# A state-space scan stage: step sizes formed in the product's PSUM bank, side jobs moved to other units, more products shared with GpSimd

## The chip, the core and the metric

The kernel runs on one core of a Trainium2 chip. A core has a matrix engine (TensorE, PE in the profile; PEld is its weight load), a vector engine (VectorE, DVE), an activation engine (ScalarE, ACT), GpSimd (POOL) and SyncE (SP), which here only issues DMAs. Each works through its own queue in order and waits on semaphores for the others. SBUF is the large on-chip memory; PSUM has eight banks of 2 KB per partition, and TensorE writes only there. The metric is the device time of one execution in microseconds; here the median of three was 3026.71 (3026.7 to 3028.8).

## The reference

The program is a decoder of two layers over 16 blocks of 128 tokens with 512 features; each of its six parts is followed by a residual sum and a layer norm. The change touches only the first part, a selective state-space scan over every block:

```python
A = -jnp.exp(A_log)                                                        # 512 x 16
dt = jax.nn.softplus(jnp.einsum('bld,ed->ble', x, dt_proj_w) + dt_proj_b)  # step sizes
bc = jnp.einsum('bld,ed->ble', x, x_proj_w) + x_proj_b
Bs, Cs = (bc[..., :d_state], bc[..., d_state:])                            # 16 and 16

def step(h, inputs):
    xt, dtt, Bt, Ct = inputs
    dA = jnp.exp(dtt[..., None] * A)
    dBx = (dtt * xt)[..., None] * Bt[:, None, :]
    h = dA * h + dBx
    y = jnp.einsum('bdn,bn->bd', h, Ct)
    return (h, y)
...
return jnp.einsum('bld,md->blm', y, out_proj_w) + out_proj_b
```

The parts after it (cross attention, ternary feed-forward, causal attention, a second cross attention, a mixture of experts) are the same in both kernels.

## The kernel before, in words

`stage_ssm` does the scan with features on the partitions: 512 features are four chunks (KC = 4) of 128 partitions, and two blocks of 128 tokens form a pair of TQ = 256 tokens. There are eight pairs, and in each 16 units, one for each state n; `units` counts u = 16 p + n. A tile of a unit is 128 x 1024 in 32 bits. One unit is

- `widths_in`: SP fetches `BC`, the rows of B and C of the state, spread over all partitions (four units ahead; six buffers)
- `decays`: ACT writes exp(dt A) into a PSUM tile `h` of two banks (a small copy of zeros and four activations, one unit ahead; two buffers, so four banks)
- `terms`: GpSimd forms `dBx` = dtx * B (two units ahead; three buffers)
- `scan`: DVE scans along the tokens. In an own unit it scans `h` in place and multiplies with C into `hC` (three buffers). In a shared unit (`shared`) it scans into `hs` in SBUF (two buffers), and GpSimd multiplies with C
- `add`: TensorE adds hC or hs, turned, into two banks `py` (eight transposes against the identity); for an own unit one unit later, for a shared unit two units later

Around them each pair does side jobs at fixed units n. For the next pair: `widths` (product `pb` for B and C, one bank), `widths_out` (ACT adds the bias, a DMA takes it to HBM), and for each half h of the features `step_product` (product `pd` in a bank), `step_exp`, `step_one`, `step_log` (ACT), `step_rest` (DVE) and `step_sum` (GpSimd), which form softplus as max(z, 0) + log(1 + e^-|z|) with a correction of the rounding of 1 + e^-|z|. For the pair behind: `sums_out` (ACT copies `py` to yT at n = 0), `turn_back` (PE), `turned_out` (ACT), `output` (PE product `po`) and `output_sum` (DVE). And `keys_values`: 64 products `pkv` on TensorE of keys and values for later stages, each copied by ACT and sent to HBM one unit later (`keys_values_out`). pb, pd, pt, po and pkv share the last two banks, "A" and "B", one tile each at a time.

In the loop over units everything is recorded through `pinned` (line 66 in the profile), which keeps the program's order on each engine: the order within an engine is that in which the code stands. The code before the loop, which forms the step sizes of the first pair, is ordered by the scheduler of the framework except for what `keep` holds.

Of the kernel before, what the change touches and what calls it, by code (L numbers as in the profile page):

```python
# [20 lines left out]
P = 128  # L21
# [86 lines left out]
def stage_ssm(k):  # L108
# [9 lines left out]
    with ExitStack() as ctx:  # L118
# [36 lines left out]
        for h in range(2):  # L155
            es = slice(2 * h * P, (2 * h + 2) * P)
            nc.scalar.dma_start(dtw[:, :, es], a["dtwT"][:, es].rearrange("(c p) e -> p c e", p=P))
        for whole, row in zip(wholes, rows):

            left = wk.tile([65, D], F32, tag="BC", name="left", bufs=6)  # L160
            nc.gpsimd.tensor_copy(row, whole)
            nc.gpsimd.tensor_tensor(left, whole, row, ALU.subtract)
            for r in (32, 64):
                nc.gpsimd.tensor_copy(row[r : r + 1], left[r : r + 1])
            nc.gpsimd.tensor_tensor(left[64:65], left[64:65], row[64:65], ALU.subtract)
            nc.gpsimd.tensor_copy(row[64:65], left[64:65])

# [25 lines left out]

        def step_product(st, h, which="A"):


            st.pd[h] = bank(which, [P, 2, TQ], "pd")
            for e in range(2):
                at = (2 * h + e) * P
                for c in range(KC):  # L200
                    q.nc.tensor.matmul(st.pd[h][:, e], dtw[:, c, at : at + P], st.xT[:, c], start=c == 0, stop=False)
                q.nc.tensor.matmul(st.pd[h][:, e], rows[0][:, at : at + P], ones, start=False, stop=True)

        def step_exp(st, h, room=None):
            if room is None:
                v = wk.tile([P, 2, TQ], F32, tag="sp_v", name="sp_v", bufs=1)
                u = wk.tile([P, 2, TQ], F32, tag="sp_u", name="sp_u", bufs=1)
            else:
                v, u = room[:, 0:2], room[:, 2:4]
            st.vu[h] = v, u  # L210
            q.nc.scalar.activation(v, st.pd[h], AF.Abs)
            q.nc.scalar.activation(v, v, AF.Exp, scale=-1.0)

        def step_one(st, h):
            v, u = st.vu[h]
            q.nc.scalar.activation(u, v, AF.Identity, bias=1.0)

        def step_rest(st, h):
            v, u = st.vu[h]
            q.nc.vector.scalar_tensor_tensor(v, u, 1.0, v, ALU.subtract, ALU.subtract)  # L220
            q.nc.vector.scalar_tensor_tensor(v, st.pd[h], 0.0, v, ALU.max, ALU.subtract)

        def step_log(st, h):
            q.nc.scalar.activation(st.dt[:, 2 * h : 2 * h + 2], st.vu[h][1], AF.Ln)

        def step_sum(st, h):
            hs = slice(2 * h, 2 * h + 2)
            q.nc.gpsimd.tensor_tensor(st.dt[:, hs], st.dt[:, hs], st.vu[h][0], ALU.add)
            q.nc.gpsimd.tensor_tensor(st.dtx[:, hs], st.dt[:, hs], st.xT[:, hs], ALU.mult)

# [89 lines left out]

        shared = lambda u: u % 8 in (1, 4, 6)

# [26 lines left out]
        for p, st in enumerate(states):  # L349
            st.p, st.h, st.BC, st.dBx, st.hC, st.pd, st.vu, st.yT, st.pt, st.y = p, {}, {}, {}, {}, {}, {}, {}, {}, {}  # L350
        first = states[0]
        widths(first, xT0)
        widths_out(first)
        room = wk.tile([P, KC, TQ], F32, tag="hC", name="room", bufs=3)
        for step in (step_product, step_exp, step_one, step_rest, step_log, step_sum):
            for h in range(2):
                step(first, h, *{step_product: ["AB"[h]], step_exp: [room if h else None]}.get(step, []))
        for _ in range(2):
# [12 lines left out]
        for u, (st, n) in enumerate(units):  # L371
# [65 lines left out]
            if n in (7, 11) and nxt:  # L437
                step_log(nxt, n // 11)
        last = states[-1]
# [1646 lines left out]
```

## Time and profile before

| What | Value |
| --- | --- |
| median of three runs | 3026.71 us |
| profiled execution, and its span | 3033.7 us, 3031.8 us |
| busy in the span | PE 97%, DVE 63%, POOL 49%, ACT 45% |
| scan stage | first scan at 29.66 us, last pair's yT at 512.74 us |
| chain that ended last, whole span | PE 67%, DVE 13%, ACT 3%, POOL 1% |
| groups of the scan stage | `decays` activation x508, 477 ns; own scans x80, 2290 ns; shared scans x48, 2282 ns; `hC` products x79, 1225 ns |
| `dt` and `dtx` on GpSimd (`step_sum`) | x14 each, 1271 and 1270 ns |

The profile is that of one execution. Busy time counts an engine's instructions; idle time is put down to the event that ended it. A group's row names the line, the engine, the operation, output <- input, the shape and the count, then busy microseconds and the mean in nanoseconds of one, then idle time before them and what ended it. A timeline row has the start, the duration in microseconds (merged where instructions of one kind follow each other), and in brackets the idle time before it.

### The profile page before, as it was taken

The numbers are of one execution on the slowest core, as the hardware profiler recorded it, in microseconds if no ns is written. First come the engines' busy times: TensorE is split into PE (matmuls) and PEld (weight loads), VectorE is DVE, ScalarE is ACT, GpSimd is POOL, SyncE is SP. The second block draws the span as 40 slices with busy tenths as digits, with TensorE's granted clock in tenths as the row PEclk, the third lists the DMA queues.
The fourth block names the chain that finished last, engine by engine and source line by source line (L and its number), as shares of the span: only waits on it lengthen the run. The fifth ranks groups of instructions, "written<-read, shape, count | busy, mean of one in ns | idle before, by whom it ended". The sixth has DMA issues, their size and how long they took to land.

```text
span 3031.8 us, 40699 instructions
## 1 busy us (share of the span) xinstructions
PE 2927.2 (97%) x13744; PEld 1830.9 (60%) x13744; DVE 1920.5 (63%) x4221; ACT 1356.5 (45%) x3315; POOL 1490.4 (49%) x1274
## 2 busy tenths in 40 slices
PE   8999999999999999999999999999999999999998
PEld 6666665455555555555787556666566666666665
DVE  6989998766776676665887897567643322242224
ACT  5776775333343343345344797655433322222221
POOL 8999996534334334332333663356435553333331
PEclk9999999999999999999999999999999999999999
DMA  6654444880000000024000200234357665555541
GB/s 199 205 138 126 121 126 135 266 285 14 8 11 11 8 11 11 8 66 143 1 1 1 70 1 8 64 115 164 136 174 241 221 226 164 165 192 165 164 150 61
DMA packets 171603, 331.58 MB, mean 109 GB/s; under 512 B 22078, under 2 KB 80958, under 8 KB 169852
## 3 DMA queue, kind: packets, MB, share of 16 engines
q1 hardware_dynamic: 126988, 219.91, 23.9%
q0 software_dynamic: 19200, 64.16, 6.3%
q10 hardware_dynamic: 25200, 44.84, 3.9%
q8 instruction: 111, 1.82, 0.2%
q14 instruction: 104, 0.85, 0.1%
HBM read 244.57 MB, written 137.43 MB: 126 GB/s over the span
## 4 chain that ended last, share of the span: by engine, by line
PE 67%; DVE 13%; ACT 3%; POOL 1%; issue 1%; DMA 1%; SPq 0%; another core or an unknown queue 0%; DVEq 0%; ACTq 0%; POOLq 0%
PE y L1830 8%; PE pu L1813 7%; PE pg L1813 7%; PE pq L676 7%; PE po L796 6%; PE po L1008 4%; PE ao L785 3%; PE sc L745 3%; PE pt L536 2%; PE pg L988 2%; PE pu L988 2%; PE pT L773 1%; PE ptx L536 1%; PE pkv L66 1%; PE pw L1482 1%
## 5 line engine op out<-in xcount | busy, mean ns | idle before, releaser
L765 POOL TENSOR_TENSOR pr<-pr,sm 128x512 f32<-128x512 f32 x128 | 135.4, 1058 | 369.2 <-DVE sm L764 273.8
L66 POOL TENSOR_TENSOR dBx<-dtx,BC 128x1024 f32<-128x1024 f32 x126 | 298.6, 2394 | 1.0 <-DMA BC<-bcd 0.4
L1813 PE MATMUL pg<-gu,xgT 128*128 128x352 f32 x784 | 297.1, 461 | 1.4 <-ACT act L1816 1.4
L1813 PE MATMUL pu<-gu,xgT 128*128 128x352 f32 x784 | 296.9, 460 | 0.0
L758 ACT ACTIVATE pr<-sc,mx,sf 128x256 f32<-128x256 f32 x256 | 142.2, 560 | 332.8 <-DVE mx L751 304.7
L1817 DVE SCALAR_TENSOR_TENSOR act<-pu,row,act 128x352 f32<-128x352 f32 x98 | 57.1, 582 | 358.4 <-PE pu L1813 339.2
L1830 PE MATMUL y<-dn,aT 128*128 128x512 f32 x588 | 268.3, 592 | 0.0
L1858 POOL TENSOR_TENSOR x<-got,x 128x512 f32<-128x512 f32 x120 | 151.7, 1270 | 225.8 <-DMA got<-results,gidx 224.6
L66 ACT ACTIVATE h<-dt,negA 128x254 f32<-128x254 f32 x508 | 242.2, 477 | 16.9
L796 PE MATMUL po<-w,aT 128*128 128x512 f32 x512 | 233.1, 593 | 1.9 <-DVE aT L790 1.9
L676 PE MATMUL pq<-w,xT 128*128 128x512 f32 x512 | 230.8, 593 | 0.6 <-DVE m L642 0.6
L1851 POOL DMA_INDIRECT got<-results,gidx x120 | 116.2, 969 | 227.6 <-DMA results<-yo 200.5
L66 DVE TENSOR_TENSOR_SCAN h<-h,dBx 128x1024 f32<-128x1024 f32 x80 | 183.2, 2290 | 34.3 <-ACT h L66 24.9
L1813 PEld LDWEIGHTS pu<-gu,xgT 128*128 128x128 f32 x784 | 149.3, 191 | 83.0 <-issue 0.5
L1816 ACT ACTIVATE act<-pg 128x352 f32<-128x352 f32 x98 | 45.5, 464 | 304.5 <-PE pg L1813 265.3
L1813 PEld LDWEIGHTS pg<-gu,xgT 128*128 128x128 f32 x784 | 141.6, 191 | 65.1 <-ACT act L1816 1.9
L647 POOL TENSOR_TENSOR m<-m,m 128x512 f32<-128x512 f32 x96 | 122.5, 1276 | 111.3 <-DVE m L642 108.0
L66 PE MATMUL pkv<-w,cT 128*128 128x512 f32 x384 | 171.6, 593 | 1.4 <-ACT y L66 1.1
L1842 DVE COPY yo<-y 128x512 f32<-128x512 f32 x90 | 62.2, 691 | 165.4 <-PE y L1830 157.9
L1830 PEld LDWEIGHTS y<-dn,aT 128*128 128x128 f32 x588 | 104.1, 190 | 100.8 <-issue 94.2
L1805 ACT COPY xgT<-ptx 128x512 f32<-128x512 f32 x98 | 57.4, 586 | 235.9 <-PE ptx L536 221.4
L998 POOL TENSOR_TENSOR lo<-sg,hi 128x512 fp32r<-128x512 f32 x64 | 84.2, 1316 | 155.4 <-ACT hi L997 155.3
(413 smaller groups left out, 6792.0 us busy)
## 6 DMA issues: line engine op xcount, KB each, us to landing
bucket<-zeros SPq DMA_DIRECT2D x96, 388.0 KB
row<-bucket SPq DMA_DIRECT2D x90, 388.0 KB
BC<-bcd SPq DMA_DIRECT2D x128, 256.0 KB
results<-yo ACTq DMA_DIRECT2D x90, 256.0 KB
gu<-in_moe_guT SPq DMA_DIRECT2D x16, 1408.0 KB
x_k<-kv ACTq DMA_DIRECT2D x32, 256.0 KB
x_v<-kv ACTq DMA_DIRECT2D x32, 256.0 KB
v<-x_v SPq DMA_DIRECT2D x32, 256.0 KB
```

What stands on the lines that cost most here:

```text
L66: return self.tc.keep_in_program_order(call(*args, **kw))
L647: nc.gpsimd.tensor_tensor(m1, m1, m2, ALU.add)
L676: nc.tensor.matmul(ps, src[:, c], w[c], start=c == 0, stop=c == KC - 1)
L758: nc.scalar.activation(pr[:, j], st.sc[g, i][:, j], AF.Exp, scale=st.sf[:, h : h + 1], bias=st.mx[g, i][:, j : j + 1], accum_out=sm[:, j : ...
L765: nc.gpsimd.tensor_tensor(pr, pr, sm.unsqueeze(2).to_broadcast([P, 2, 2 * P]), ALU.mult)
L796: nc.tensor.matmul(st.po, aT[:, j], k.wo[h // 8][:, h % 8], start=h == 0, stop=h == G * J - 1)
L988: nc.tensor.matmul(p[:, e], w[:, c, at : at + P], sn.qT[:, :, c], start=c == 0, stop=c == KC - 1)
L1008: nc.tensor.matmul(sn.po[i], part[:, e, i * P : (i + 1) * P], k.fd[hc // 8][:, hc % 8], start=hc == 0 and part is parts[0], stop=hc == 15 ...
L1813: nc.tensor.matmul(ps, u.xT[:, c], gu[:, c, lo : lo + I], start=c == 0, stop=c == KC - 1)
L1830: self.nc.tensor.matmul(u.y, u.aT[:, c], u.w[1][:, c], start=c == 0, stop=c == 2)
L1851: nc.gpsimd.indirect_dma_start(out=got[:, :], out_offset=None, in_=k.results[h][g][0:end, :], in_offset=bass.IndirectOffsetOnAxis(ap=self. ...
L1858: nc.gpsimd.tensor_tensor(k.x[b], got, k.x[b], ALU.add)
```

## The change

`step_exp` keeps m = max(z, 0) and u = |z| in SBUF and writes e^-|z| over the product in its PSUM bank; the sums that follow stay in that bank. `step_sum` moves from GpSimd to DVE, and `step_out` copies dt from the bank to SBUF with ACT. Seven of 16 units are shared instead of six, at other places. Side jobs stand at other units, and the banks of `keys_values` change with them. `step_log` now follows `step_one` in its unit or two units later. Before the loop, one of the two bias rows is split on DVE, 26 products of ones are issued on TensorE, and the first pair's step sizes are formed in four quarters (`first_steps`). The core of the diff:

```diff
+        warm = bank("B", [P, 2, TQ], "warm")
+        for _ in range(26):
+            nc.tensor.matmul(warm[:, 0], ones[:, 0:P], ones, start=True, stop=True)
-        for whole, row in zip(wholes, rows):
+        for engine, whole, row in zip((nc.vector, nc.gpsimd), wholes, rows):
...
-            nc.gpsimd.tensor_copy(row, whole)
-            nc.gpsimd.tensor_tensor(left, whole, row, ALU.subtract)
+            engine.tensor_copy(row, whole)
+            engine.tensor_tensor(left, whole, row, ALU.subtract)
...
-        def step_product(st, h, which="A"):
+        def step_product(st, h):
-            st.pd[h] = bank(which, [P, 2, TQ], "pd")
+            st.pd[h] = bank("A", [P, 2, TQ], "pd")
...
-        def step_exp(st, h, room=None):
-            if room is None:
-                v = wk.tile([P, 2, TQ], F32, tag="sp_v", name="sp_v", bufs=1)
-                u = wk.tile([P, 2, TQ], F32, tag="sp_u", name="sp_u", bufs=1)
-            else:
-                v, u = room[:, 0:2], room[:, 2:4]
-            st.vu[h] = v, u
-            q.nc.scalar.activation(v, st.pd[h], AF.Abs)
-            q.nc.scalar.activation(v, v, AF.Exp, scale=-1.0)
+        def step_exp(st, h):
+            m = wk.tile([P, 2, TQ], F32, tag="sp_m", name="sp_m", bufs=1)
+            u = wk.tile([P, 2, TQ], F32, tag="sp_u", name="sp_u", bufs=1)
+            st.mu[h] = m, u
+            q.nc.scalar.activation(m, st.pd[h], AF.Relu)
+            q.nc.scalar.activation(u, st.pd[h], AF.Abs)
+            q.nc.scalar.activation(st.pd[h], u, AF.Exp, scale=-1.0)
 
         def step_one(st, h):
-            v, u = st.vu[h]
-            q.nc.scalar.activation(u, v, AF.Identity, bias=1.0)
+            q.nc.scalar.activation(st.mu[h][1], st.pd[h], AF.Identity, bias=1.0)
+
+        def step_log(st, h):
+            q.nc.scalar.activation(st.dt[:, 2 * h : 2 * h + 2], st.mu[h][1], AF.Ln)
 
         def step_rest(st, h):
-            v, u = st.vu[h]
-            q.nc.vector.scalar_tensor_tensor(v, u, 1.0, v, ALU.subtract, ALU.subtract)
-            q.nc.vector.scalar_tensor_tensor(v, st.pd[h], 0.0, v, ALU.max, ALU.subtract)
-
-        def step_log(st, h):
-            q.nc.scalar.activation(st.dt[:, 2 * h : 2 * h + 2], st.vu[h][1], AF.Ln)
+            m, u = st.mu[h]
+            q.nc.vector.scalar_tensor_tensor(st.pd[h], u, 1.0, st.pd[h], ALU.subtract, ALU.subtract)
+            q.nc.vector.tensor_tensor(st.pd[h], m, st.pd[h], ALU.subtract)
 
         def step_sum(st, h):
             hs = slice(2 * h, 2 * h + 2)
-            q.nc.gpsimd.tensor_tensor(st.dt[:, hs], st.dt[:, hs], st.vu[h][0], ALU.add)
-            q.nc.gpsimd.tensor_tensor(st.dtx[:, hs], st.dt[:, hs], st.xT[:, hs], ALU.mult)
+            q.nc.vector.tensor_tensor(st.pd[h], st.dt[:, hs], st.pd[h], ALU.add)
+            q.nc.vector.tensor_tensor(st.dtx[:, hs], st.pd[h], st.xT[:, hs], ALU.mult)
+
+        def step_out(st, h):
+            q.nc.scalar.copy(st.dt[:, 2 * h : 2 * h + 2], st.pd[h])
+
+        def first_steps(st, c, room):
+            h, e = divmod(c, 2)
+            if e == 0:
+                st.pd[h] = bank("AB"[h], [P, 2, TQ], "pd")
+            pd, (m, u) = st.pd[h][:, e], [r[:, c] for r in room]
+            at = c * P
+            for i in range(KC):
+                nc.tensor.matmul(pd, dtw[:, i, at : at + P], st.xT[:, i], start=i == 0, stop=False)
+            nc.tensor.matmul(pd, rows[0][:, at : at + P], ones, start=False, stop=True)
+            nc.vector.tensor_scalar(m, pd, 0.0, None, ALU.max)
+            nc.scalar.activation(u, pd, AF.Abs)
+            nc.scalar.activation(pd, u, AF.Exp, scale=-1.0)
+            nc.scalar.activation(u, pd, AF.Identity, bias=1.0)
+            nc.scalar.activation(st.dt[:, c], u, AF.Ln)
+            nc.vector.scalar_tensor_tensor(pd, u, 1.0, pd, ALU.subtract, ALU.subtract)
+            nc.vector.tensor_tensor(pd, m, pd, ALU.subtract)
+            nc.vector.tensor_tensor(st.dt[:, c], st.dt[:, c], pd, ALU.add)
+            nc.gpsimd.tensor_tensor(st.dtx[:, c], st.dt[:, c], st.xT[:, c], ALU.mult)
...
-        shared = lambda u: u % 8 in (1, 4, 6)
+        shared = lambda u: u % 16 in (4, 6, 7, 8, 12, 13, 14)
...
-        room = wk.tile([P, KC, TQ], F32, tag="hC", name="room", bufs=3)
-        for step in (step_product, step_exp, step_one, step_rest, step_log, step_sum):
-            for h in range(2):
-                step(first, h, *{step_product: ["AB"[h]], step_exp: [room if h else None]}.get(step, []))
+        room = [wk.tile([P, KC, TQ], F32, tag="hC", name="room", bufs=3) for _ in range(2)]
+        for c in range(KC):
+            first_steps(first, c, room)
...
+                if n in (8, 14):
+                    step_out(nxt, n // 14)
...
+                if n in (6, 12):
+                    step_log(nxt, n // 12)
...
-            if n in (4, 8) and back:
-                output_sum(back, n // 8)
-            if n in (7, 11) and nxt:
-                step_rest(nxt, n // 11)
-            if n in (8, 13) and nxt:
+            if n in (6, 9) and back:
+                output_sum(back, n // 9)
+            if n in (6, 12) and nxt:
+                step_rest(nxt, n // 12)
+            if n in (7, 13) and nxt:
                 step_sum(nxt, n // 13)
...
-                if n in (3, 7):
-                    output(back, n // 7)
+                if n in (5, 8):
+                    output(back, n // 8)
...
-            at = {5: "B", 9: "B", 11: "B", 12: "A", 13: "B", 14: "A", 15: "B"}
+            at = {2: "B", 6: "B", 9: "B", 11: "B", 12: "B", 14: "B", 15: "A"}
             if not back:
-                at |= {0: "A", 1: "B", 3: "B", 7: "B"}
+                at |= {0: "B", 1: "A", 4: "B", 7: "B"}
             if not nxt:
-                at |= {2: "A", 4: "A", 8: "A"}
+                at |= {4: "A", 7: "A", 10: "A"}
...
-            if n in (7, 11) and nxt:
-                step_log(nxt, n // 11)
```

`step_exp` stays at n = 5 and 9, `step_one` at 6 and 10, `step_product` at 4 and 8, `widths` at 2, `widths_out` at 3.

More of the change, by code (lines that the diff above doesn't have):

```diff
@@ L157, in stage_ssm @@
             nc.scalar.dma_start(dtw[:, :, es], a["dtwT"][:, es].rearrange("(c p) e -> p c e", p=P))
-        for whole, row in zip(wholes, rows):
+        warm = bank("B", [P, 2, TQ], "warm")
+        for _ in range(26):
+            nc.tensor.matmul(warm[:, 0], ones[:, 0:P], ones, start=True, stop=True)
+        for engine, whole, row in zip((nc.vector, nc.gpsimd), wholes, rows):
             left = wk.tile([65, D], F32, tag="BC", name="left", bufs=6)
-            nc.gpsimd.tensor_copy(row, whole)
-            nc.gpsimd.tensor_tensor(left, whole, row, ALU.subtract)
+            engine.tensor_copy(row, whole)
+            engine.tensor_tensor(left, whole, row, ALU.subtract)
             for r in (32, 64):
-                nc.gpsimd.tensor_copy(row[r : r + 1], left[r : r + 1])
-            nc.gpsimd.tensor_tensor(left[64:65], left[64:65], row[64:65], ALU.subtract)
-            nc.gpsimd.tensor_copy(row[64:65], left[64:65])
+                engine.tensor_copy(row[r : r + 1], left[r : r + 1])
+            engine.tensor_tensor(left[64:65], left[64:65], row[64:65], ALU.subtract)
+            engine.tensor_copy(row[64:65], left[64:65])
         negA = cst.tile([P, KC, NS], F32, name="negA")
@@ L349, in stage_ssm @@
         for p, st in enumerate(states):
-            st.p, st.h, st.BC, st.dBx, st.hC, st.pd, st.vu, st.yT, st.pt, st.y = p, {}, {}, {}, {}, {}, {}, {}, {}, {}
+            st.p, st.h, st.BC, st.dBx, st.hC, st.pd, st.mu, st.yT, st.pt, st.y = p, {}, {}, {}, {}, {}, {}, {}, {}, {}
         first = states[0]
```

## The prediction

> **What bounds it now.** The change lies in the first 513 us, so I read the busy times by stretch first, the groups by shape of that stretch second, and the timelines of ACT, DVE and PE last.
>
> ```profile
> core 0: us, PE busy (x) PEld busy (x) DVE busy (x) ACT busy (x) POOL busy (x), PEclk, DMA share, GB/s
> 300.00:400.00 100.00, 92.93 (x482) 63.13 (x483) 90.80 (x55) 71.47 (x164) 92.63 (x44) 1.00 0.42 129
> 400.00:500.00 100.00, 96.86 (x506) 66.32 (x506) 91.27 (x54) 70.19 (x162) 93.34 (x42) 1.00 0.42 119
> ```
>
> Three engines are over 90% busy; none of them alone is the bound.
>
> ```profile
> L66 POOL TENSOR_TENSOR dBx<-dtx,BC 128x1024 f32<-128x1024 f32 x126 | 298.6, 2394 | 1.0 <-DMA BC<-bcd 0.4
> L66 POOL TENSOR_TENSOR hs<-hs,BC 128x1024 f32<-128x1024 f32 x48 | 113.2, 2358 | 18.9 <-DVE hs L66 18.8
> L66 DVE SCALAR_TENSOR_TENSOR sp_v<-sp_u,sp_v 128x512 f32<-128x512 f32 x14 | 30.5, 2181 | 0.0
> L66 DVE SCALAR_TENSOR_TENSOR sp_v<-pd,sp_v 128x512 f32<-128x512 f32 x14 | 9.7, 692 | 1.5
> L66 DVE TENSOR_TENSOR x<-po,x 128x512 f32<-128x512 f32 x14 | 9.4, 674 | 0.0
> ...
> 416.94 4.21 DVE L66 SCALAR_TENSOR_TENSOR sp_v<-sp_u,sp_v 128x512 f32<-128x512 f32 x1
> 435.09 0.82 DVE L66 SCALAR_TENSOR_TENSOR sp_v<-sp_u,sp_v 128x512 f32<-128x512 f32 x1
> ```
>
> One operation with both inputs in SBUF takes 0.82 us or 4.21, by what GpSimd does beside it; the same size with an input in PSUM takes 0.69 and 0.67.
>
> ```profile
> 94.94 1.08 ACT L66 COPY yT<-py 128x512 f32<-128x512 f32 x2 [0.72 <-PE py L66]
> 393.53 1.07 ACT L66 COPY yT<-py 128x512 f32<-128x512 f32 x2 [0.72 <-PE py L66]
> 454.08 1.07 ACT L66 COPY yT<-py 128x512 f32<-128x512 f32 x2 [0.72 <-PE py L66]
> 512.74 1.07 ACT L233 COPY yT<-py 128x512 f32<-128x512 f32 x2 [0.72 <-PE py L344]
> ...
> 397.28 1.91 PE L66 MATMUL pb<-xT,xpw 128*32 128x256 f32 x8 [1.09 <-ACT y L66]
> 422.00 1.99 PE L66 MATMUL pd<-xT,w 128*128 128x256 f32 x8 [1.44 <-DVE sp_v L66]
> 33.27 1.97 PE L66 MATMUL py<-ident,hC 128*128 128x128 f32 x8 [5.08 <-DVE hC L66]
> ```
>
> yT marks the end of a pair. The six middle pairs take (454.08-94.94)/6 = 59.86 us: the other marks (153.46, 211.82, 272.51, 332.95) make two of about 58.4 and four of 60.6, those with the 4.21. PE's work in one, by the distance of neighbouring starts: 16 `add` of 0.873, 7 `keys_values` of 3.43, two `output` of 3.66, two `step_product` of 3.69, turn-back and `widths` 1.75 each: 56.2, about 56.5 with the split form of `keys_values` (3.58). So PE idles 3.3 us of a pair; 1.44 and 1.09 are the largest waits. PE is the floor, and no version of this scan can save more than its gaps.
>
> **The change, GpSimd and DVE.** Per pair GpSimd now issues 16 `terms`, 6 shared products and four halves of 1.31: 22 x 2.33 + 5.2 = 56.5 and the stretching by the 4.21. After: 23 x 2.33 = 53.6. DVE: an own unit costs 3.51 (scan to scan), a shared one 2.20. Before, 10 x 3.51 + 6 x 2.20 + two `output_sum` of 0.58 + `step_rest` (2 x 0.69 and 4.21 + 0.82, less overlap) = 55.5. After, 9 x 3.51 + 7 x 2.20 + 1.2 + eight operations with one operand in PSUM, which come in dependent pairs of 1.38: 53.7. These eight shapes are not in the trace; nearest are the rows of 0.69 and 0.67, and I take them. If instead one of them met GpSimd as the two-SBUF form does, 8 x 3.4 = 27 us a pair would be the other end; each has an operand in PSUM, as both short rows have, so I keep it out.
>
> **ACT.** A `decays` occupies 2.13, and the next scan starts 2.27 after its first copy. `keys_values_out` costs 0.99, not 0.58, as its DMA issue waits for its copy. `step_exp` has three activations (1.73 for 1.16), `step_out` is new (0.52), `step_log` moves. Sum 16 x 2.13 + 7 x 0.99 + 2 x (1.73 + 1.16 + 0.52) + yT, y, bc 2.8 = 50.6, on average free. Relu and Abs are taken at the 0.59 of Abs from PSUM; at zero or twice that, two Relu move ACT by 1.1 a pair, of which the layout below lets at most half reach DVE.
>
> **A middle pair laid out.** Averages don't decide here; the order on each engine is fixed, so I laid the rows end to end with each wait, from scan(6) = 0, PE 3.15 behind. In the new order scan(8) needs the `hs` buffer of 6 (two buffers), so PE's add(6); scan(14) needs add(12). ACT: decays(7) 0.35, one and log to 3.66. DVE: `step_rest` 3.16, scan(7) 4.54, `step_sum` 6.74, scan(8) 8.12 (add(6) done at 7.6: no wait). PE: keys_values(6) 3.15 to 6.58, output(1) from 7.45, when its bank is copied, products to 14.80, keys_values(9) to 19.1. ACT's step_exp(1) thus starts at 15.0, decays(11) is late, scan(11) at 19.0 instead of 17.9, scan(12) at 23.1. scan(14) waits for add(12) until 30.55; scan(0) of the next pair 36.4, yT 39.66. PE starves once: add(1) waits for hC(1) until 43.58, 1.3 us, in place of the 1.09 for y. `widths` to 46.2, keys_values(2) to 49.6, scan(5) at 53.94 after bc, keys_values(6) again at 60.57. That is 57.4 for the pair; GpSimd is never later than DVE wants. Bank A is now held by pd until `step_out` has read it: product(1) may start at 10.5 and PE comes to it at 11.1, keys_values(15) at 33.4 and 34.6, so this costs nothing while PE is behind; a PE 0.6 us earlier would wait. With split forms 57.65: 2.2 less than 59.86, six times: **-13.2**. The `step_product` wait of 1.44 is gone, since 0.69 follows one; late next is DVE behind ACT behind `keys_values_out`.
>
> DMAs: none is added. `BC` of unit 14 is requested when hs(8) frees its buffer (14.1) and used at 21.4; unit 20's 37.2 and 44.1. The longest landing on the chain of waits is 5.61, so 1.3 to spare; SP holds the weight pieces behind it, whose users come after the scan.
>
> **The start.** 26 warm-up matmuls cover 1.3 to about 7, under the wait for xT (7.76); pb then takes 1.9 for 3.59. But negA now stands behind bc on ACT, and DVE's rows behind negA, so the bias row is there at about 13.5 (12.64 before). The quarters do not run one behind the other: in the built order c0 and c2 come first, one in each bank, and the product of c1 waits until DVE has finished c0, c3 until c2. Laid out with 0.39 per activation and 0.36 per DVE step (halves of the 512 rows, plus their fixed part): c0 complete 18.3, c1's product to 20.25, c3's to 22.1, c3 complete 26.1, scan(0) 29.2 (29.66 before). Yet bank B is free for the first keys_values only at 26.1 (20.36 before), which puts add(0) at 34.0 (33.27): the 5.08 us of idle are filled by work that came earlier, not saved.
>
> Row on the clock: after those 5.08 idle us the granted clock was 0.50 from 32 to 36, and the eight transposes took 1.97 for 1.04. The new waits of about 4.4 and 3.9 lie between this row and the 1.4 us that cost no clock; I take full speed, and 2 us more (1 for each) as the other end. The Trainium skill, TensorE: Matmul & The Clock Gate, Part 1, has one idle window of about 3.4 us put the clock back to half; the row of 5.08 agrees. By it both gaps can undo the warm-up, and the sum would be 2 us worse.
>
> **First and last pair.** The first has ten keys_values after add(0). Numbers 6 and 7 now share bank B, with no PE work between; the copy of 6 stands behind `decays`(8) and that behind exp, one and log: 3.7 us of PE idle (58.7 to 62.4). yT at 96.3, +1.3 on 94.94. The last pair has ten and no steps. PE: scan(8) waits for add(6) behind keys_values 6 and 7; then keys_values(9) waits 2.1 for output_sum(1), add(3) 1.8, add(1) 1.3: 62.4 instead of 58.66, +3.7. Bounds: 0 if DVE gets its lead back, 5 if the waits of the first pair recur.
>
> **Sum.** +1.3 - 13.2 + 3.7 = -8.2. Nothing behind the scan changes, and PE heads the chain at its end, so it passes on whole. The profiled execution (3033.7, span 3031.8) would be 3025.5; it is 7.0 above the median of the runs, to which I apply the sum: 3018.5.
>
> **Rivals.** (1) The bunched shared units cost nothing at both ends, for DVE leads there by more than I laid out: only the 13.2, 3013.5. For it: DVE and GpSimd lose 2 and 3 us of work a pair, PE none. Against: two `hs` buffers. If PE's gaps vanished altogether, 6 x 3.3 + 1.2 + 3.8 = 24.8, 3002, the utmost. (2) Half of the middle gain is lost to ACT, each 0.5 us of which moves DVE where PE starves: 58.8 a pair, -6.4 + 5, 3025, no change that can be told. (3) Slower: the two `hs` buffers bind in each pair as in the last, so that DVE waits for PE at scan(8) and PE for DVE at keys_values(9); 3.7 more a pair, 61.4, six times +1.5, and 5 at the ends: +14, 3041. It decides from a middle pair of 59.0 up. For it: scan(8) has 0.5 us to spare. Against: PE is 3 us behind, and has output and product to fill the time. The quarters failing to overlap is in the forecast.
>
> **Chances.** Forecast 0.44, (1) 0.20, (2) 0.23, (3) 0.13. 0.2% (6 us) is about what can be told from no change. A quarter of the forecast's spread (3014 to 3023) lies above 3020.7: faster 0.53, same 0.34, slower 0.13. The range takes in (1), (2) and the 2 us of clock: 3008 to 3030.
>
> **To check.** yT marks 57 to 58 apart in the middle, over 61 in the last pair; DVE steps at 0.6 to 0.7; add(1), not pb, waiting; keys_values(7) waiting some 4 us in the first pair; scan(0) near 29. A DVE step of 2 us or more, or middle marks of 59, makes the prediction wrong.

## The result, and the profile after

The changed kernel takes 3037.74 us (median of eight runs, 3034.4 to 3041.4) against 3026.94 (eight runs of the kernel before, 3019.44 to 3031.05): a ratio of 1.0038, 95% interval 1.0027 to 1.0049. It is slower by some 11 us; 3018.5 was predicted, with 3008 to 3030 as the range. The profiled execution took 3041.4 us, the longest of the eight, its span 3039.6.

The yT marks in the timeline of ACT show where the time went (start, duration, engine, line, operation; the idle time before it in brackets). Before, the same marks stood at 94.94, 153.46, 454.08 and 512.74:

```profile
107.83 1.08 ACT L66 COPY yT<-py 128x512 f32<-128x512 f32 x2 [0.53 <-PE py L66]
169.48 1.07 ACT L66 COPY yT<-py 128x512 f32<-128x512 f32 x2 [0.40 <-ACT kv L66]
459.22 1.07 ACT L66 COPY yT<-py 128x512 f32<-128x512 f32 x2 [0.53 <-PE py L66]
523.74 1.07 ACT L255 COPY yT<-py 128x512 f32<-128x512 f32 x2 [0.72 <-PE py L366]
```

| Stretch | Before | After | Difference | Predicted |
| --- | --- | --- | --- | --- |
| start to add(0) | 33.27 | 42.97 | +9.7 | +0.7 |
| add(0) to yT of the first pair | 61.67 | 64.86 | +3.2 | +0.6 |
| second pair | 58.52 | 61.65 | +3.1 | as a middle pair |
| third to seventh pair, together | 300.62 | 289.74 | -10.9 | -11 |
| last pair | 58.66 | 64.52 | +5.9 | +3.7 |
| yT of the last pair | 512.74 | 523.74 | +11.0 | -8.2 |

(The -11 is five of the six times 2.2 that were predicted.) So the scan does gain where it was said to, and nearly as much: 57.95 us a pair from the third to the seventh, 57.65 laid out. It gives back twice that at both ends. The rest of the program, which is the same, took 2515.9 us after the last yT in this execution and 2519.1 in that of before; over all the profiled executions below it lies between 2511.3 and 2524.7, a spread of 13 us in code that is the same. The marks are therefore the sharper measure, but of one execution each; the ratios go by medians of several, and the two can differ by some 5 us.

The busy times by stretch and the groups by shape of the first 505 us answer to those shown of before:

```profile
300.00:400.00 100.00, 98.58 (x500) 66.68 (x499) 92.16 (x62) 78.56 (x180) 93.09 (x41) 1.00 0.50 130
400.00:500.00 100.00, 93.67 (x476) 62.52 (x475) 87.88 (x57) 71.34 (x165) 91.38 (x41) 0.98 0.48 126
```

```profile
L66 POOL TENSOR_TENSOR dBx<-dtx,BC 128x1024 f32<-128x1024 f32 x125 | 293.0, 2363 | 17.1 <-DVE h L66 10.2 <-DMA BC<-bcd 7.0
L66 POOL TENSOR_TENSOR hs<-hs,BC 128x1024 f32<-128x1024 f32 x53 | 125.2, 2363 | 33.3 <-DVE hs L66 31.2 <-PE py L66 2.1
L66 DVE TENSOR_TENSOR pd<-sp_m,pd 128x512 f32<-128x512 f32 x14 | 9.7, 696 | 0.5
L66 DVE TENSOR_TENSOR dtx<-pd,xT 128x512 f32<-128x512 f32 x14 | 9.7, 692 | 0.5
L66 DVE SCALAR_TENSOR_TENSOR pd<-sp_u,pd 128x512 f32<-128x512 f32 x14 | 9.6, 685 | 4.6 <-ACT sp_u L66 4.5
L66 DVE TENSOR_TENSOR pd<-dt,pd 128x512 f32<-128x512 f32 x14 | 9.4, 672 | 0.0
```

PE (the first column) is now 98.6% busy between 300 and 400, against 92.9% before: most of the gaps in the middle are gone. (The stretch from 400 to 500 takes in 41 us of the last pair.) The four VectorE steps of the step sizes take 0.67 to 0.70 each, all 56 of them. GpSimd now waits for DMA BC, which it hardly did before (7.0 us for 0.4); that belongs to the second pair, below.

The timeline of PE at the start holds most of the loss:

```profile
1.22 5.73 PE L160 MATMUL warm<-ones 65*128 65x256 bf16 x26 [1.22 <-DVE zero L175]
8.24 3.59 PE L187 MATMUL pb<-xT,xpw 128*32 128x256 f32 x8 [1.29 <-DMA alog<-in_A_log]
11.76 4.91 PE L241 MATMUL pd<-xT,w 128*128 128x256 f32 x16
17.84 0.39 PE L242 MATMUL pd<-ones,rows_dtb 65*128 65x256 bf16 x2 [1.18 <-DVE rows_dtb L169]
22.05 3.78 PE L241 MATMUL pd<-xT,w 128*128 128x256 f32 x8 [3.81 <-DVE dt L250]
...
32.06 6.70 PE L304 MATMUL pkv<-cT,w 128*128 128x128 f32 x32 [3.22 <-DVE dt L250]
39.44 3.70 PE L66 MATMUL pkv<-w,cT 128*128 128x512 f32 x8 [0.68 <-ACT kv L313]
42.97 1.04 PE L66 MATMUL py<-ident,hC 128*128 128x128 f32 x8
```

The same timeline of before has, of these,

```profile
7.76 3.59 PE L184 MATMUL pb<-xT,xpw 128*32 128x256 f32 x8 [7.76 <-DMA xT<-in_xT]
20.36 3.84 PE L282 MATMUL pkv<-cT,w 128*128 128x128 f32 x32 [0.47 <-DVE room L221]
```

pb takes 3.59 us as it did before: the warm-up changed nothing. The bias row comes at 17.84. The second quarter (c1; the quarters are c0 to c3, and c0 and c2 come first) waits for the first (3.81), and then runs at half speed, 3.78 for eight products that elsewhere take 1.89. The product of keys (pkv, L304) takes 6.70, where before it took 3.84. The same code does not always lose as much: add(0), after the same start, stood at 42.97, 39.10, 40.82, 40.08, 42.33 and 41.88 in six profiled executions (this one, e6, e7, e8, e12, e13), and the keys product varied from 3.84 to 6.70. The +9.7 is the largest of the six, their mean +7.9.

### The profile page after: what moved, and what is told of

Same layout as the page of the kernel before. It is cut to its first block, busy times and chain, and to the rows that moved or that the text cites. A ratio compares the mean times of both kernels' runs of the same rounds, so it can differ in the third digit from the quotient of the medians.

```text
span 3039.6 us, 40770 instructions
## 1 busy us (share of the span) xinstructions
PE 2939.5 (97%) x13770; PEld 1840.3 (61%) x13770; DVE 1913.4 (63%) x4259; ACT 1371.8 (45%) x3351; POOL 1467.3 (48%) x1248
## 4 chain that ended last, share of the span: by engine, by line
PE 67%; DVE 12%; ACT 2%; issue 1%; POOL 1%; DMA 1%; SPq 0%; DVEq 0%; ACTq 0%; POOLq 0%
PE y L1853 8%; PE pg L1836 8%; PE pu L1836 7%; PE pq L699 7%; PE po L819 6%; PE po L1031 4%; PE ao L808 3%; PE sc L768 3%; PE pt L559 2%; PE pg L1011 2%; PE pu L1011 2%; PE pT L796 1%; PE ptx L559 1%; PE pw L1505 1%; PE ps L1420 1%
## 5 line engine op out<-in xcount | busy, mean ns | idle before, releaser
L66 DVE TENSOR_TENSOR_SCAN h<-h,dBx 128x1024 f32<-128x1024 f32 x72 | 165.0, 2292 | 30.6 <-ACT h L66 26.8
```

The source lines that it names most:

```text
L66: return self.tc.keep_in_program_order(call(*args, **kw))
```

## The experiments

Each group ran on one chip beside the kernel before, and each ratio is to its own runs of the kernel before. Times are those of each kernel's profiled execution; "five pairs" is the mean of the third to the seventh.

| Kernel | first scan | add(0) | yT, first | second pair | five pairs | last pair | yT, last | ratio (95%) |
| --- | --- | --- | --- | --- | --- | --- | --- | --- |
| before | 29.66 | 33.27 | 94.94 | 58.52 | 60.12 | 58.66 | 512.74 | 1 |
| changed | 35.28 | 42.97 | 107.83 | 61.65 | 57.95 | 64.52 | 523.74 | 1.0038 (1.0027-1.0049) |
| e1 | 29.06 | 32.68 | 99.92 | 61.61 | 57.97 | 62.82 | 514.20 | 1.0018 (1.0007-1.0030) |
| e2 | 34.19 | 38.08 | 99.77 | 57.97 | 60.13 | 58.66 | 517.07 | 1.0015 (1.0005-1.0025) |
| e3 | 31.22 | 43.45 | 108.31 | 62.22 | 57.95 | 64.52 | 524.82 | 1.0034 (1.0020-1.0048) |
| e4 | 32.14 | 38.60 | 103.47 | 62.16 | 57.95 | 64.51 | 519.90 | 1.0030 (1.0018-1.0043) |
| e6 | 34.27 | 39.10 | 101.88 | 59.19 | 58.00 | 64.51 | 515.60 | 1.0026 (1.0014-1.0037) |
| e7 | 34.36 | 40.82 | 105.68 | 60.52 | 58.05 | 58.66 | 515.09 | 1.0018 (1.0008-1.0027) |
| e8 | 33.63 | 40.08 | 104.95 | 59.17 | 58.01 | 62.82 | 516.98 | 1.0025 (1.0015-1.0035) |
| e9 | 28.85 | 32.46 | 98.66 | 63.53 | 57.97 | 62.80 | 514.85 | 1.0023 (1.0013-1.0032) |
| e10 | 26.43 | 36.50 | 101.36 | 62.82 | 58.00 | 64.51 | 518.71 | 1.0015 (1.0006-1.0025) |
| e11 | 31.00 | 42.98 | 108.00 | 64.38 | 57.95 | 62.83 | 524.95 | 1.0034 (1.0022-1.0046) |
| e12 | 34.82 | 42.33 | 108.07 | 60.77 | 59.05 | 60.37 | 524.46 | 1.0038 (1.0024-1.0052) |
| e13 | 34.38 | 41.88 | 106.30 | 62.26 | 58.34 | 62.82 | 523.07 | 1.0037 (1.0026-1.0047) |
| b1 | 28.91 | 32.52 | 99.07 | 58.16 | 57.97 | 58.66 | 505.76 | 0.9959 (0.9945-0.9972) |
| b2 | 26.96 | 31.33 | 92.77 | 58.84 | 57.97 | 58.65 | 500.13 | 0.9947 (0.9933-0.9961) |

### The start: e1 to e4

e1 puts the changed loop behind the start of before; e2 the changed start ahead of the loop of before; e3 takes the warm-up out; e4 forms both bias rows on GpSimd again.

```diff
 e3
-        for _ in range(26):
-            nc.tensor.matmul(warm[:, 0], ones[:, 0:P], ones, start=True, stop=True)
 e4
-        for engine, whole, row in zip((nc.vector, nc.gpsimd), wholes, rows):
+        for engine, whole, row in zip((nc.gpsimd, nc.gpsimd), wholes, rows):
```

> The changed loop behind the start of before (bias rows split on GpSimd, no warm-up, step sizes of the first pair in two halves with SBUF operands). Theory S, the start is what lost: the first add on PE comes near 33.3 us instead of 42.97, and the loop then takes about the 481 us that it took in the changed kernel, so the last yT lies near 514 and the time near 3028. Rival L, the loop itself lost (first, second and last pair), and the late start would have been made up: the time stays above 3034.

> The mirror: the start of the changed kernel ahead of the loop of before. Theory S: the first add comes some 9.5 us later than before, all of which lasts to the last yT (about 522), time near 3036. Rival L: the old loop makes up for most of it, as its first pair has gaps on PE to give; time near 3029.

> The changed kernel without the 26 products of ones. If the warm-up did nothing (the first product of xT ran at 630 ns an instruction with it and without it), the start and the time are those of the changed kernel, 3037 to 3038, with the products of the first step sizes still slow at first. If it did shorten the slow time, the first add comes 2 us or more later than 42.97, and the time is near 3040.

> The changed kernel with both bias rows split on GpSimd, as before. If the split on DVE beside GpSimd is what made the bias row late (ready at 17.8 instead of 12.7), the first bias product comes near 14.5, all that follows 3 us earlier, and the time is near 3034.5. If the wait of negA behind bc, or the clock, sets the start anyway, add(0) moves by under 1 us, and the time stays at 3037.

With the old start (e1) add(0) comes at 32.68, 10.3 us earlier, and 9.5 of these are still there at the last yT. The ratio falls from 1.0038 to 1.0018 only, about 6 us; the two intervals do not exclude 9.5, and it would fit as well if the execution shown above lost more in its start than the median run did. e2 shows the new start alone: +4.8 at add(0), where 9.5 was expected, and +4.3 at the last yT. In e2 the keys product ran at full clock (3.84). In the changed loop, with the keys product at 3.84 as well (e6), add(0) stands at 39.10, 1.0 later, since keys_values 0 waits there 0.68 us for the copy out of bank B; the rest of the 42.97 is the clock. e3: pb takes 3.59 without the warm-up as with it, and the ratio is no worse (1.0034), so the warm-up was worth nothing. e4: with both rows on GpSimd the bias product comes at 15.68, 2.2 us earlier than with the two engines side by side. Its add(0) is 4.4 us earlier than that of the changed kernel and 2.6 earlier than the mean of the six; what lies between 2.2 and 4.4 is the clock (c3 and the keys product took 2.89 and 6.70 us in the changed kernel, 1.89 and 5.46 in e4).

Why two engines are slower than one is in the timelines of DVE, of the changed kernel and of e3, where GpSimd happened to form its row later (at 14.86, after VectorE had done):

```profile
12.62 0.68 DVE L165 TENSOR_TENSOR left<-whole,rows_dtb 65x512 f32<-65x512 f32 x1
13.22 0.22 DVE L1994 CAST identb<-ident 128x128 bf16<-128x128 f32 x1
13.45 2.03 DVE L167 CAST rows_dtb<-left 1x512 bf16<-1x512 f32 x2
15.52 0.98 DVE L168 TENSOR_TENSOR left<-left,rows_dtb 1x512 f32<-1x512 f32 x1
16.53 1.26 DVE L169 CAST rows_dtb<-left 1x512 bf16<-1x512 f32 x1
```

```profile
9.76 0.85 DVE L164 CAST rows_dtb<-left 1x512 bf16<-1x512 f32 x2
10.64 0.68 DVE L165 TENSOR_TENSOR left<-left,rows_dtb 1x512 f32<-1x512 f32 x1
11.36 0.42 DVE L166 CAST rows_dtb<-left 1x512 bf16<-1x512 f32 x1
```

The same three operations on one partition take 4.3 us beside GpSimd and 2.0 alone. They also begin 3.7 us earlier in e3: the order of the code before the loop came out otherwise there (and in e11), with negA on ScalarE at 8.52, ahead of bc, where the changed kernel has it at 12.24, behind bc. So e3 differs from the changed kernel in more than the warm-up. It gains 4 us at its first scan (31.22 for 35.28), yet none at add(0): its keys product waits 3.60 us for the copy of the one before in bank B and then takes 6.54 us at half clock.

### The warm-up: e9 and e11

Fifteen f32 products of a tile of ones over all 128 rows take the place of the 26 bf16 products over 65 rows: in e9 ahead of the old start, in e11 ahead of the changed one.

```diff
+        full = wk.tile([P, KC, TQ], F32, tag="hs", name="full")
+        nc.vector.memset(full[:, 0], 1.0)
+        for _ in range(15):
+            nc.tensor.matmul(warm[:, 0], full[:, 0, 0:P], full[:, 0], start=True, stop=True)
```

> The changed loop behind the start of before (as in e1), with 15 f32 products of a tile of ones over all 128 rows ahead of everything in place of the 26 bf16 products over 65 rows. If rows and passes decide whether the clock rises, pb takes 1.9 us in place of 3.59, the step sizes come some 1.5 us earlier, the first scan at 27.5 (29.06 in e1), and the ratio is 0.0005 under e1's 1.0018. If such a burst ahead of the first loads doesn't raise the clock at all, pb stays at 3.6, the first scan at 29 and the ratio at 1.0018.

> The changed kernel with its warm-up done as in e9 (15 f32 products over 128 rows) and nothing else altered. Theory: the warm-up then speeds pb (1.9 us), but the start is held by the bias row and by c1 waiting for c0, in which waits the clock falls again, so the first add stays at 39 to 43 us and the ratio at 1.003 to 1.004. Rival: the slow clock was what the start lost, and with it gone the first add comes 3 us or more earlier than any of 39.1 to 43.0.

The timeline of PE of e9:

```profile
1.49 8.18 PE L162 MATMUL warm<-full 128*128 128x256 f32 x30 [1.49 <-DVE zero L177]
9.60 1.91 PE L189 MATMUL pb<-xT,xpw 128*32 128x256 f32 x8
11.44 1.99 PE L206 MATMUL pd<-xT,w 128*128 128x256 f32 x8
```

Now the clock rises (an instruction of these products goes from 634 to 379 ns at 4.4 us, 2.9 us after the first began) and pb takes 1.91. But the first scan gains 0.2 us only, because it waits for GpSimd's dtx and dBx (5.21 us of idle VectorE), not for TensorE. In e11 all is as in e3: the second quarter still waits 2.88 for the first, the keys products wait 3.9 and 3.6 and fall back to half clock (5.47, 6.29), add(0) stands at 42.98. In e9 to e11 the clock that the warm-up had raised did not outlast the waits behind it.

### The quarters: e10

Each quarter has a bank to itself: the two banks of the sums, which are free until add(0), and A and B. The rows are both on GpSimd, dt and dtx are formed on VectorE in the bank, and the warm-up has 128 rows.

```diff
-            if e == 0:
-                st.pd[h] = bank("AB"[h], [P, 2, TQ], "pd")
+            if c in (0, 1):
+                pd = ps_y.tile([P, KC, P], F32, tag=f"py{c}", name="pd").rearrange("p c t -> p (c t)")[:, 0:TQ]
+            else:
+                pd = bank("BA"[c - 2], [P, 2, TQ], "pd")[:, 0]
```

> The changed loop, unaltered, behind a start with the quarters in a bank each: c0 and c1 in the two banks of the sums, c2 in B, c3 in A, so that no quarter's product waits for another's chain; bias rows both on GpSimd; the first pair's dt and dtx on VectorE in the bank; 12 f32 products over all 128 rows as warm-up. Theory (the quarters failed because two share a bank): the four products run one behind the other at full clock, c3 is done near 19, its chain near 21.5, the first scan comes at 24 to 25 in place of 35.3, the first add at 30 to 32 in place of 43.0 (some of it lost to keys_values 0 in bank B), the last yT at 511 to 513, and the ratio to before is 0.999 to 1.0. Rival: the quarters are paced by GpSimd, the landing of BC or ScalarE anyway, and the first scan stays at 29 or later.

The first scan comes at 26.43 (35.28; 29.66 before). The quarters' products now run end to end, 10.55 to 18.2. The chain of the last quarter, with ScalarE and VectorE still busy with those before it, ends at 23.9 in place of 21.5, and dBx takes 2.35 more. So the theory held for TensorE, and the rival for the last 2 us; add(0), the last yT (518.71) and the ratio (1.0015) all came out worse than expected. The 8.9 us are those of four alterations together (banks, rows, dtx on VectorE, warm-up), which were not tried apart. Of them 6.5 reach add(0):

```profile
22.75 5.25 PE L308 MATMUL pkv<-cT,w 128*128 128x128 f32 x32 [4.57 <-ACT dt L255]
31.26 5.40 PE L66 MATMUL pkv<-w,cT 128*128 128x512 f32 x8 [3.27 <-ACT kv L317]
```

The second row is keys_values 0 of the loop: it waits 3.27 us for the copy out of bank B and then runs at half clock. Moved to bank A (in b2, same start), it follows at once with 3.60 us, and add(0) comes at 31.33 in place of 36.50: the bank of this one product costs 5.2 us.

### The first and the last pair: e6 and e7

e6 lays the first pair's keys_values differently; e7 gives the last pair its old shared units, places and banks.

```diff
 e6
-                at |= {0: "B", 1: "A", 4: "B", 7: "B"}
+                at = {0: "B", 1: "A", 3: "B", 5: "B", 7: "B", 9: "B", 11: "B", 12: "B", 13: "B", 14: "B", 15: "A"}
 e7
+        shared = lambda u: u % 8 in (1, 4, 6) if u >= len(units) - NS else u % 16 in (4, 6, 7, 8, 12, 13, 14)
...
+                at = {2: "A", 4: "A", 5: "B", 8: "A", 9: "B", 11: "B", 12: "A", 13: "B", 14: "A", 15: "B"}
```

> The changed kernel, with only the first pair's keys_values laid differently: at units 0, 1, 3, 5, 7, 9, 11, 12, 13, 14 and 15 (still eleven), so that no two of them stand in bank B with nothing for TensorE between. Theory: the copy of number 6 that stands behind decays cost 3.53 us of idle TensorE and, by the clock that fell in it, 1.7 more on the next product (5.47 for 3.73): add(0) to yT of the first pair goes from 64.9 to about 60, all later marks come some 5 us earlier, and the ratio to the kernel before is about 1.002. Rival: the four shared units in a row with two hs buffers hold VectorE anyway, so the pair stays at 64 and the wait shows up at another place.

> The changed kernel, with only the last pair laid as in the kernel before: shared units 1, 4 and 6 of every 8, output at 3 and 7, output_sum at 4 and 8, and its ten keys_values at 2, 4, 5, 8, 9, 11 to 15. The step sizes have no work in the last pair, so if the bunched units and their places are what costs, its 64.5 us from yT to yT become 58.7 as before, and the ratio is about 1.002. Rival: TensorE enters the last pair with a different lead and loses the same at other waits: 62 to 64 stay, and the ratio stays at 1.0035 to 1.004.

In the changed kernel the timeline of PE had, in the first pair, the wait of keys_values 7 for the copy of number 6, and in the last one the wait for output_sum(1), each with the half-speed product that followed:

```profile
71.71 5.47 PE L66 MATMUL pkv<-cT,w 128*128 128x128 f32 x32 [3.53 <-ACT kv L66]
...
494.30 5.40 PE L66 MATMUL pkv<-w,cT 128*128 128x512 f32 x8 [1.99 <-DVE x L66]
```

e6 takes the first of them away, but the pair gains 2.1 us (62.78 from add(0) to yT), not 5. Next in line stands the product of the second half, in the timeline of PE of e6:

```profile
68.37 1.99 PE L66 MATMUL pd<-xT,w 128*128 128x256 f32 x8 [3.25 <-ACT dt L66]
```

It waits for bank A, which the first half's pd holds until ACT has copied dt. In the changed kernel this wait was 0.79, hidden behind the other. The rival (VectorE holds the pair) is not what the trace shows either: VectorE waits there for TensorE (5.02 us for an `hs` buffer), not TensorE for it.

e7 settles the last pair: 58.66, to the digit as before. (Of what it wins back, 1.7 us are the clock: 62.8 is what the pair takes in the runs where the same wait of 2.0 us was followed by a product of 3.70.)

### The second pair: e8

In the changed kernel `widths` of the second pair (pb, for the pair after it) waits in the timeline of PE (first fence); the releaser that is named, h of ACT, does not feed it, and pb's only late input is xT:

```profile
114.20 1.89 PE L66 MATMUL pb<-xT,xpw 128*32 128x256 f32 x8 [1.57 <-ACT h L66]
```

```profile
100.73 1.77 SPq L582 DMA_DIRECT2D w<-in_xa_wqT  x1
102.61 0.78 SPq L66 DMA_DIRECT2D xT<-in_xT  x1
```

The second fence is SyncE's queue: xT is requested 5.2 us ahead of the mark at 107.83; before it was requested at 87.13, 7.8 us ahead of the mark at 94.94, and had 11.6 us until pb. From 105 to 115 the DMA engines are over 95% busy, with pieces of the query weights, BC, and keys and values on their way out. e8 asks for the query weights eight units later:

```diff
-            if u >= 6:
+            if 6 <= u < 14 or u >= 22:
                 next(pieces, None)
```

> The changed kernel, with the eight pieces of the query weights (512 KB each, on SyncE's queue) requested at units 22 to 29 in place of 14 to 21. Theory on the second pair: there xT, requested at 102.6 behind a piece, lands near 114.2 and holds widths for 1.57 us; with it keys_values(2), the bias of bc behind its copy, decays(5) and the scan of unit 5 (4.29 us idle against 1.6 in a middle pair) come late. Then the second pair takes 58 to 58.5 in place of 61.65, and the ratio falls to about 1.0027. Rival: what the first pair left over (its late VectorE) is the cause, and the pair stays above 61.

The pair takes 59.17, pb waits for nothing, and VectorE stands idle for 1.56 us before the scan of unit 5, where it was 4.29. So the pieces are what the pair lost by; but xT is only one of two ways, and not the one that ended last. Behind the bias of bc, ScalarE has to request the write of bc, and `decays`(5) comes after that. The timelines of ACT of the changed kernel and of e4:

```profile
120.75 0.47 ACT L66 ACTIVATE bc<-pb,xpb 32x256 f32<-32x256 f32 x1 [0.40 <-DMA BC<-bcd]
122.72 0.17 ACT L66 COPY h<-zero 128x8 f32<-128x8 f32 x1 [1.50 <-DMA w<-in_xa_wqT]
```

```profile
114.77 0.46 ACT L66 ACTIVATE bc<-pb,xpb 32x256 f32<-32x256 f32 x1 [0.41 <-DMA BC<-bcd]
118.37 0.17 ACT L66 COPY h<-zero 128x8 f32<-128x8 f32 x1 [3.14 <-DMA w<-in_xa_wqT]
```

The request waits until a piece of the query weights has landed: in the trace it waits on a semaphore to which that piece reports too. In e8 the same idle time is 0.40, with no piece in it. In e4 pb does not wait at all, and yet VectorE stands idle for 4.32 us before the scan of unit 5 and the pair takes 62.16: so far as e4 tells, an earlier xT alone would have won next to nothing in the changed kernel. In other runs pb's wait is the last (e9, e11, e13), and in e10 the profile even names its releaser (timeline of PE):

```profile
107.90 3.44 PE L66 MATMUL pb<-xT,xpw 128*32 128x256 f32 x8 [1.75 <-DMA xT<-in_xT]
```

The rival is not out altogether: e6, which alters the first pair only, also brings the second to 59.19, with neither wait; there xT is requested 8.6 us ahead of the mark.

### What the middle pairs gain from: e12 and e13

e12 returns the shared units of before in every pair; e13 returns one operation with two SBUF inputs per half (and drops ScalarE's Relu).

```diff
 e12
-        shared = lambda u: u % 16 in (4, 6, 7, 8, 12, 13, 14)
+        shared = lambda u: u % 8 in (1, 4, 6)
 e13
-            q.nc.scalar.activation(st.pd[h], u, AF.Exp, scale=-1.0)
+            q.nc.scalar.activation(m, u, AF.Exp, scale=-1.0)
...
-            q.nc.vector.scalar_tensor_tensor(st.pd[h], u, 1.0, st.pd[h], ALU.subtract, ALU.subtract)
-            q.nc.vector.tensor_tensor(st.pd[h], m, st.pd[h], ALU.subtract)
+            q.nc.vector.scalar_tensor_tensor(m, u, 1.0, m, ALU.subtract, ALU.subtract)
+            q.nc.vector.scalar_tensor_tensor(st.pd[h], st.pd[h], 0.0, m, ALU.max, ALU.subtract)
```

> The changed kernel with the shared units of before (1, 4 and 6 of every 8, six in a pair) and all else of the change. It asks which part gave the middle pairs their 2 us. If the step sizes and the places of the side jobs gave them, a middle pair stays at 57.9 to 58.3. If the seventh shared unit is needed (VectorE's work per pair by the prediction's sums 55 for 53.7), it rises to 59 or more, five pairs by 5 us or more. The last pair tells whether the bunching of shared units there cost the 5.9 us, or output and keys_values at their new places: 58.7 to 60 in the first case, over 62 in the second.

> The changed kernel with one VectorE operation per half of the step sizes taking both inputs from SBUF again: e^-|z| stays in SBUF, (1 + e) - 1 - e is formed there, and max(z, 0) minus it goes to the bank as before; the Relu on ScalarE falls away. All other places are those of the change. If an operation with two SBUF inputs beside GpSimd takes 4.2 us, as in four of six middle pairs of before, a middle pair rises from 57.9 to 60 to 61. If the places of the side jobs gave the gain, the pair stays at 58, whatever the operation takes.

With six shared units a middle pair takes 59.05: the seventh, with its places, is worth 1.1 of the 2.2 us. In the last pair e12 gives back 4.2 of the 5.9, of which 1.7 are the clock: the bunching of shared units is most of what the change loses there, and output, output_sum and keys_values at their places the other 1.7. In e13 the timeline of DVE shows the operation that took 4.21 and 0.82 us in the kernel before:

```profile
306.28 2.43 DVE L66 SCALAR_TENSOR_TENSOR sp_m<-sp_u,sp_m 128x512 f32<-128x512 f32 x1
...
329.00 0.67 DVE L66 SCALAR_TENSOR_TENSOR sp_m<-sp_u,sp_m 128x512 f32<-128x512 f32 x1
```

At its new place it takes 2.43 and 0.67, and the pair 58.34: 0.4 more, not 2 to 3. So the bank as such is worth 0.4 us, with one operation less on ScalarE, and neither theory was right to its number. If the parts add up, the rest, some 0.7, is left for the new places and for the sums that moved from GpSimd to VectorE; these two were not tried apart.

### Put together: b1 and b2

b1 is the changed loop with the old start, e6's first pair, e7's last pair and e8's query weights. b2 has e10's start, keys_values 0 in bank A, and the first pair's second half product in bank B, so that it need not wait for the first half.

> The changed loop behind the start of before, with the first pair's keys_values of e6, the last pair of e7 and the query weights of e8. If the parts add up: first add 32.7, first pair 62.8, second 58 to 59.2, the five after it 57.95 each, last 58.7, so the last yT at about 502.5 (512.74 before), and a ratio of 0.9965 to 0.998. If each loss only moves to another place when one is mended, the last yT stays above 508 and the ratio at 0.999 or more.

> As b1, with the start of e10 (quarters in four banks, warm-up over 128 rows), and the first pair's second half product in bank B with keys_values at 0, 1, 3, 5, 6, 9 and 11 to 15, so that this product needn't wait for the first half's bank (3.25 us in e6). If that holds, first add at 28 to 30, first pair 60 to 61, the others as in b1: last yT near 496, ratio 0.994 to 0.996. If ScalarE's order holds the first pair anyway, it stays at 62.8 and the ratio is 0.996 to 0.997.

The marks of b2, in the timeline of ACT:

```profile
92.77 0.59 ACT L66 COPY yT<-py 128x512 f32<-128x512 f32 x1 [0.72 <-PE py L66]
...
441.48 1.07 ACT L66 COPY yT<-py 128x512 f32<-128x512 f32 x2 [0.53 <-PE py L66]
500.13 1.08 ACT L259 COPY yT<-py 128x512 f32<-128x512 f32 x2 [0.72 <-PE py L370]
```

b1 ends the scan at 505.76 (502.5 expected; its first pair takes 66.5 from the earlier add(0), as 3.23 us of wait for bank A and two half-speed stretches remain), b2 at 500.13 (496). Against the kernel before they measure 0.9959 (0.9945 to 0.9972) and 0.9947 (0.9933 to 0.9961): by the ratios 12 and 16 us faster, by the marks 7 and 13. The parts add up to within 3 to 4 us of the expected marks, and the scan as changed is good for a gain once its ends are mended.

## Why the prediction was wrong

**Right.** The VectorE steps at 0.67 to 0.70; the middle pair, 57.95 for 57.65 laid out, with add(1) waiting 1.04 (1.3) and the stall of 1.44 gone; the wait of keys_values 7 in the first pair, 3.53 (3.7); in the last pair scan(8) held for 6.46 us by add(6), keys_values(9) waiting 1.99 (2.1), add(3) 1.64 (1.8), add(1) 1.05 (1.3). Reading the order on each engine and laying rows end to end carried far.

The last yT was to come 8.2 us earlier and came 11.0 later. Of these 19.2 us the start has 9.0, the first pair 2.6, the second 5.3, the last 2.2, the five between 0.1.

**Where it failed: the start.** It was to cost 0.7 us at add(0) and cost 9.7 in the profiled execution (7.9 on average over six with this start). Three terms of that step were wrong.
- The bias row: at 13.5 predicted, at 17.8 measured, 4.3 us. That it stands behind negA was right (its subtraction began at 12.62). But the operations after it were taken short (at the speed of e3 they would have ended at 15.5, 2.0 us later than predicted), and in the changed kernel they run beside GpSimd's row and are stretched, by 2.3 more. The profile of before had the warning, the 4.21 for 0.82, and it was applied to the scan and not to the start.
- The clock: full speed was taken, with 2 us as the other end. Measured: 1.9 on c1 (3.78 for 1.89), 1.0 on c3 (2.89), 2.9 on the keys product (6.70 for 3.84), 5.8 in all. (The two terms make 10.1; the chains of c0 and c3 took some 1 us less than laid out.) The row that decides it, 5.08 idle us and then 1.97 for 1.04, was in hand, and so was the rule of the Trainium skill, quoted there; the value taken was the wrong end, and even that end was too low: it gave 1 us to each of the two waits, which cost 2.9 each.
- The warm-up was taken to give pb 1.9 us. No row of before showed that such products raise the clock; they did not, and e9 shows which would. This cost the sum nothing, for pb was not what the start waited for.

That the quarters would not overlap, and that bank B delays the first keys_values, was in the forecast, and the traces of the changed kernel, e10 and b2 agree with both.

**The second pair was not laid out at all.** It was counted as a middle pair, 57.65, and took 61.65. The DMA step looked at BC against its landing and put the weight pieces aside, as their users come after the scan; it did not ask what else waits for them. xT did, behind them in SyncE's queue, and so did ScalarE's request for the write of bc: together 2.5 us by e8, of the 3.1.

**First and last pair: the mechanism right, the size off.** Each had one more term, the clock after the wait: 5.47 for 3.73, and 5.40 for 3.70, 1.7 us each. Where the clock held in the last pair, in e1, e8, e9, e11 and e13, it took 62.8, 4.2 more than before (3.7 predicted); 4.2 and 1.7 make the 5.9. And "costs nothing while PE is behind", said of bank A, did not hold in the first pair, where PE is ahead (0.79; 3.25 in e6).

**The rivals.** The slower one gave 3041, near the time measured, but for another reason: it had the two hs buffers bind in each pair, with 61.4 a pair, and the pairs take 57.95. In those the scan of a shared unit waits for TensorE's sums by 0.5 to 0.65 us; the buffers bind at the ends, by 4.84 us in the first pair and 6.46 in the last.

## What to carry to other kernels

A change to a loop in steady state has to be laid out for its first, second and last rounds too: there the engines lead and lag differently, other jobs fill the banks, and other transfers share the queue; here the ends lost 22 us and the middle won 11. A wait of TensorE of 2 us or more, as these were, should be priced twice, once as idle and once as the half-speed product that may follow. A prefetch has to be checked against everything that waits behind it, on its own queue and on others. And work moved to a second engine to share the load has to be priced as it runs beside the first.

## What the runs showed of the hardware

- In each of the sixteen traces the changes of the granted clock lie whole multiples of 3.41 us apart; in the changed kernel it rises at 14.20, falls at 21.03, rises at 27.86, falls at 31.27 and rises at 38.10.
- 26 bf16 products over 65 rows, 5.73 us without a break, left the clock where it was in all eight executions that have them; f32 products over 128 rows raised it in 2.9 (e9) to 3.8 us (e10, b2). Bad luck with the 3.41 us is not the reason: in six of the eight a whole such interval lay within the bf16 products (in e6 from 1.84 to 5.25, counted back from the rise at 12.08). Rows and type were not tried apart. The Trainium skill (TensorE: Matmul & The Clock Gate, Part 1) gives some 3.4 us of sustained work as what raises it, with no word of its kind; the runs here depend on the kind.
- The same wait of 2.0 us in the last pair cost the clock in some executions (5.40 in the changed kernel) and not in others (3.70 in e8), and the keys product after 3.2 to 3.4 us of wait took 3.84, 5.47 or 6.70 with the same code. The grid of 3.41 us, which a wait meets at another place in each execution, would explain this; no run sets that place.
- Three one-partition operations on VectorE took 2.0 us alone and 4.3 beside GpSimd; the two-SBUF operation took 0.67 or 2.43 (e13), 0.82 or 4.21 (before), by its place.
